# Another assignment of the model dimension to partitions in a gated cross-attention kernel

## The chip, the cores and the metric

The kernel runs on one core of a Trainium2 chip. Its time is what the device takes for one execution, in microseconds (us); lower is better. A core has five engines with their own instruction queues: PE (TensorE, matrix products), DVE (VectorE), ACT (ScalarE), POOL (GpSimd) and SP (SyncE, which here issues nearly all transfers). [...] DMA engines, sixteen to a core, move data between the main memory and SBUF, the on-chip memory of 128 partitions. Matrix products land in PSUM, in banks.

## The reference

For each of 8 batches, x is 1024 rows of D = 1024, the context ("mem") 64 rows of E = 512. All values are float32.

```python
memory_proj = einsum('bme,de->bmd', memory, W_mem)
scores = einsum('bnd,bmd->bnm', hidden_states, memory_proj) / sqrt(D)
attn = softmax(scores, axis=-1)
memory_context = einsum('bnm,bmd->bnd', attn, memory_proj)
gate_input = concatenate([hidden_states, memory_context], axis=-1)
gate = sigmoid(einsum('bnf,df->bnd', gate_input, W_gate) + b_gate)
fused = hidden_states + gate * memory_context
return rmsnorm(fused, norm_w)
```

W_gate has two halves along f: W1, which multiplies x, and W2, which multiplies the memory context. Since the context is attn times memory_proj, the kernel multiplies memory_proj by W2 once per batch ("mg") and then only applies attn. The large product is x times W1.

## The kernel before

**Layout.** A product on PE sums over partitions. So D has to lie over 128 partitions and KD = 8 chunks, in the same way for every operand that is summed over it: x, W1, W2's rows, and memory_proj ("mp"). Before, element d of D lies on partition d // 8 in chunk d % 8. For W1 and W2 that is a plain load, since a partition's 8 rows lie one after another in memory (`rows_by_chunk`, L103). For x it needs a transpose. x is loaded by `load_xq` (L149) in four DMAs, one to each 32 partitions, so that each group of 32 holds one quarter of the columns for all 512 rows of a step. DVE then transposes blocks of 32 x 32 (`transpose_x`, L239, instruction L248), and its input takes every eighth column (`chunks`, L107), so the elements that it reads one after another are 32 bytes apart. `store_mp` (L412, instruction L418) does the same in the other direction for memory_proj, there with the output 32 bytes apart. In the product pm = W_mem times the context (L211 on), W_mem is the stationary operand and its columns are also taken eight apart.

**The start.** SP issues, in this order: the context (memq), W_mem (wm; its first 128 rows go through ACT's queue, L128), W2 in eight loads of 512 KB (L134 to L138), W1 in two of 2 MB (L144), norm_w (nw_sb), and later memory_proj's copies to memory (mpd, L404) and the first block of x (L405). PE transposes the context (L194), multiplies it by W_mem (pm), and then runs seven products for mg (pg, `mg_product`, L434) by one level of a Strassen scheme. DVE runs its own queue strictly in program order ("pin", L89). It holds, one after another: memT copies (L199), differences of W2's blocks (`w2_sum`, L389 and L390), a difference of W1's first half (`outer_sum(5, 7, 1)`, L393) with four smaller ones (L394), the copies of pm from PSUM to mpT (L400, shared with ACT), two steps on mpT (s1 and s2, L459), a difference that needs W1's second half (`outer_sum(7, 3, 7)`, L461), the eight transposes of `store_mp`, and then sums of the pg products, transposes of x's first block and more differences of W1. The sums also free PSUM banks for later products.

**The main part.** There are 16 steps q of 512 rows. Each runs seven outer products (ORDER, L527), each of seven inner products kA to kF (kA has two parts), by two levels of the same scheme. POOL and DVE form the operands and add up the results; DVE also does eight transposes for the next step, the softmax, and the gate. A table of slots (`plan`, L530) sets where each of these stands in the queues. SP loads x and stores the output.

**Helpers.** L92 issues every matmul, L95 every elementwise operation of two tensors, on whichever engine is given, and L98 every DMA of SP. So a profile line with L95 is told apart by its tile names: t_w are W2's differences, t, it and w the operands from W1, l, s and a those from x, mpT memory_proj.

Of the kernel before, what the change touches and what calls it, by code (L numbers as in the profile page):

```python
# [15 lines left out]
P = 128  # L16
# [4 lines left out]
def tile_gated_cross_attention_rmsnorm(  # L21
# [38 lines left out]

    nc = tc.nc
    B, N, D = x.shape
    M, E = mem.shape[1:]
# [3 lines left out]
    BM = B * M  # L70
    KD = D // P
    KE = E // P
    H = 512
    C = 256
    NPAIR = BM // P
# [6 lines left out]
    apool = ctx.enter_context(tc.tile_pool(name="apool", bufs=1))  # L82
# [6 lines left out]
    pin = tc.keep_in_program_order  # L89

    def mm(o, lhsT, rhs, start, stop):
        pin(nc.tensor.matmul(o, lhsT, rhs, start=start, stop=stop, skip_group_check=True))  # L92
# [4 lines left out]
    def load(o, i):  # L97
        pin(nc.sync.dma_start(o, i))  # L98

    def t4k(pool, shape, tag, name):  # L100
        return pool.tile(shape, F32, tag=tag, name=name)

    def rows_by_chunk(w, n):  # L103

        return w.rearrange("(p j) f -> p j f", j=n)

    def chunks(t, n):  # L107

        return t.rearrange("p s e -> p (s e)").rearrange("p (m j) -> p j m", j=n)

    banks = [f"b{i}" for i in range(5)]

    def bank(n, shape, name):
        return ps.tile(shape, F32, tag=banks[n % 5], name=name)
# [10 lines left out]
    memq = [t4k(rot, [P, 2, E], "l2", f"memq{i}") for i in range(2)]  # L125
    wm = t4k(xqpool, [P, KE, D], "xq", "wm")
    wmr = w_mem_t.rearrange("(k p) d -> p k d", p=P)
# [2 lines left out]
        load(memq[g], memr[g])  # L130
    load(wm[:, 1, :], wmr[:, 1, :])
    load(wm[:, 2:, :], wmr[:, 2:, :])
    w2r = rows_by_chunk(w_gate_t[D:, :], KD)
    w2 = []  # L134
    for k in range(KD):
        t = t4k(*((gpool, [P, D], "gate") if k < 7 else (apool, [P, D], "s4")), f"w2_{k}")
        load(t, w2r[:, k, :])
        w2.append(t)  # L138

    w1 = [const.tile([P, 4, D], F32, name=f"w1_{h}") for h in range(2)]
    for h in range(2):
        load(w1[h], rows_by_chunk(w_gate_t[:D, :], KD)[:, 4 * h : 4 * h + 4, :])  # L144
    nw_sb = const.tile([P, D], F32, name="nw_sb")
    load(nw_sb, norm_w.partition_broadcast(P))
    xq = {}

    def load_xq(q):  # L149
# [7 lines left out]
    outer_b = {  # L157
        o: w1[h][:, :, c * H : (c + 1) * H]
        for o, h, c in ((1, 0, 0), (7, 0, 1), (2, 1, 0), (3, 1, 1))
    }  # L160

    t_w2 = [const.tile([P, 4, H], F32, tag=f"t{o}", name=f"t{i}_w2") for i, o in ((1, 6), (2, 4))]
    inner_t = {}

    def w1_place(o):

        if o in (5, 6, 4):
            outer_b[o] = const.tile([P, 4, H], F32, tag=f"t{o}", name=f"t{o}")
        inner_t[o] = const.tile([P, 3, 2, C], F32, tag=f"it{o}", name=f"it{o}")
# [17 lines left out]
    def transpose_mem(g):  # L187

        cols = slice(g * (BM // 2), (g + 1) * (BM // 2))
        for k in range(KE):  # L190
            for r in range(2):
                n = 2 * g + r
                pin(
                    nc.tensor.transpose(  # L194
                        pt[k][:, n * P : (n + 1) * P], memq[g][:, r, k * P : (k + 1) * P], ident
                    )
                )
            o = memT[k // 2][:, k % 2, cols]
            pin((nc.scalar.copy if k % 2 else nc.vector.tensor_copy)(o, pt[k][:, cols]))  # L199

    pt = [bank(4, [P, BM], "pt0")]
    pt += [ps_ctx.tile([P, BM], F32, tag="ctx", name=f"pt{k}") for k in (1, 2)]
    pt += [ps.tile([P, BM], F32, tag="sc", name="pt3")]
    for g in range(2):
        transpose_mem(g)
    pm = [bank(j, [P, BM], f"pm{j}") for j in range(5)]
    pm += [ps_ctx.tile([P, BM], F32, tag="ctx", name=f"pm{j}") for j in (5, 6)]
    pm += [ps.tile([P, BM], F32, tag="sc", name="pm7")]
    for k in range(KE):
        for j in range(KD):  # L210
            mm(  # L211
                pm[j],
                chunks(wm[:, k : k + 1, :], KD)[:, j],
                memT[k // 2][:, k % 2, :],
                k == 0,
                k == KE - 1,
            )
# [16 lines left out]
    A, S, L2, O = {}, {}, {}, {}  # L234
# [4 lines left out]
    def transpose_x(q, t, half):  # L239

        key = q, t // 2, half
        if key not in A:
            A[key] = t4k(
                apool, [P, KH, 2 * P], f"a{t // 2 + 1}{half + 1}", f"a{t // 2 + 1}{half + 1}_{q}"
            )
        r = t % 2
        pin(
            nc.vector.transpose(  # L248
                A[key][:, :, r * P : (r + 1) * P],
                chunks(xq[q][:, 4 * t : 4 * t + 4, :], KD)[:, half * KH : (half + 1) * KH],  # L250
            )
        )

    def outer_s(q, n):
        a11, a12, a21, a22 = (A.get((q, r, h)) for r in range(2) for h in range(2))
        if n == 3:
            S[q, 3] = a21
            tt(nc.vector, a21, a11, a21, ALU.subtract)
            return
        s = S[q, n] = t4k(apool, [P, KH, 2 * P], f"s{n}", f"s{n}_{q}")  # L260
        if n == 1:
# [33 lines left out]
    def scores(q):  # L295
# [3 lines left out]
        for k in range(KD):  # L299
            for r in range(2):  # L300
                mm(
                    pst[r * M : (r + 1) * M, :],
                    mpb[:, k, :],
                    A[q, r, k // KH][:, k % KH, :],
                    k == 0,
# [65 lines left out]
    def add_bias(b):  # L371
# [1 line left out]

    KH = KD // 2
    HM = BM // 2
    b11, b12, b21, b22 = (
        [w2[h * KH + k][:, c * H : (c + 1) * H] for k in range(KH)]
        for h in range(2)  # L380
        for c in range(2)
    )
    t1, t2 = ([t[:, k, :] for k in range(KH)] for t in t_w2)

# [12 lines left out]
    mpT = [[t4k(apool, [P, KH, HM], f"a{r + 1}{h + 1}", f"mpT{r}{h}") for h in range(2)] for r in range(2)]  # L397
# [9 lines left out]
    def mp_step(eng, tag, pool, a, b, op):  # L407
        t = t4k(pool, [P, KH, HM], tag, f"mp_{tag}")
        tt(eng, t, a, b, op)
        return t  # L410

    def store_mp(g):  # L412

        r, n = g // 2, g % 2
        mpq = const.tile([P, 4, Q4], F32, tag=f"it{(4, 6, 2, 3)[g]}", name=f"mpq{g}")
        for h in range(2):
            pin(
                nc.vector.transpose(  # L418
                    chunks(mpq, KD)[:, h * KH : (h + 1) * KH],
                    mpT[r][h][:, :, n * P : (n + 1) * P],  # L420
                )
            )
        for i in range(4):
            load(
                mgd[0, g * P : (g + 1) * P, i * Q4 : (i + 1) * Q4].rearrange(
                    "(s c) e -> c s e", c=32
                ),
                mpq[32 * i : 32 * (i + 1), :, :],
            )
# [4 lines left out]
    def mg_product(n, l, r):  # L434
        nonlocal mg_next
        pgs = []
        for t in range(2):
            tag = mg_banks[mg_next % 8]
            mg_next += 1
            pg = (ps_ctx if tag == "ctx" else ps).tile([P, H], F32, tag=tag, name=f"pg{n}_{t}")  # L440
            for k in range(KH):
# [4 lines left out]
    def mg_tile(pool, tag, name):  # L446
        return t4k(pool, [P, 2, H], tag, name)

# [10 lines left out]
    s1 = mp_step(nc.vector, "s1", apool, m21, m22, ALU.add)  # L459
    s2 = mp_step(nc.vector, "s2", apool, s1, m11, ALU.subtract)  # L460
# [12 lines left out]
    for g in (2, 3, 0, 1):  # L473
        store_mp(g)
# [4 lines left out]
    for t in range(4):  # L479
        transpose_x(0, t, 0)  # L480
# [17 lines left out]
    for t in range(2):  # L498
        transpose_x(0, t, 1)
# [7 lines left out]
    for t in (2, 3):  # L507
        transpose_x(0, t, 1)
# [337 lines left out]
```

## Time and profile before

The time is 980.86 us (three runs, 980.78 to 980.89). The profiled execution spans 979.4 us.

| engine | busy us | share of the span |
|---|---|---|
| PE, matmuls | 964.8 | 99% |
| PE, weight loads | 769.8 | 79% |
| DVE | 820.4 | 84% |
| ACT | 324.9 | 33% |
| POOL | 730.5 | 75% |

| group | count | busy us | mean ns |
|---|---|---|---|
| L248 DVE transposes of x, 128x512 | 128 | 137.9 | 1098 |
| L418 DVE transposes of mp, 128x512 | 8 | 7.7 | 1101 |
| pm weight loads, 128x128 | 64 | 20.0 | 314 |

| transfer | loads | KB each | median us from issue to landing |
|---|---|---|---|
| W2 | 8 | 512 | 11.0 |
| W1 | 2 | 2048 | 15.6 |
| x | 64 | 512 | 9.6 |

The first table is over the whole span. A busy share says how much an engine works and not whether anything waits for it. What sets the end is read from the chain of waits, which follows the last instruction back to what released each step. In the second table, the mean is of the single record; records on one engine overlap a little, so the busy time is less than the count times the mean. In the third, a landing time includes the wait behind earlier transfers.

### The profile page before, as it was taken

The page shows a single profiled execution, that of the slowest core. Times are in us where ns is not written, and L with a number is a line of the kernel's source. Part 1 is how long each engine was busy: PE and PEld are TensorE (multiplying, and loading weights), DVE is VectorE, ACT ScalarE, POOL GpSimd, SP SyncE. Part 2 cuts the span into 40 slices and gives each one's busy share as a digit, 9 for nine tenths or more (in the row PEclk, how much of TensorE's full clock was granted, in tenths as well). Part 3 has the DMA queues.
Part 4 walks back from the last instruction along what each step waited for, and adds up shares of the span by engine and source line. Part 5 has one row for each costly group of instructions (what it writes and reads, how often), then busy time and mean ns, then how long its engine had stood idle before and what let it go on. Part 6 is the DMA issues. An engine that isn't in the chain of part 4 may idle for free.

```text
span 979.4 us, 14277 instructions
## 1 busy us (share of the span) xinstructions
PE 964.8 (99%) x4938; PEld 769.8 (79%) x4938; DVE 820.4 (84%) x1487; ACT 324.9 (33%) x602; POOL 730.5 (75%) x881
## 2 busy tenths in 40 slices
PE   9999999999999999999999999999999999999995
PEld 6546888888887888888887888888887888888873
DVE  3888788979797988979797988979797988979787
ACT  1100234151433334151433334151433334151434
POOL 3366877878787877878787877878787877878772
PEclk9999999999999999999999999999999999999998
DMA  9865264482918374482918374482818364482612
GB/s 372 258 153 145 39 120 107 103 188 62 186 65 165 108 141 106 102 190 65 183 65 164 111 138 105 107 184 66 182 65 168 110 136 104 108 184 68 169 65 86
DMA packets 71255, 128.32 MB, mean 131 GB/s; under 512 B 12432, under 2 KB 49296, under 8 KB 70928
## 3 DMA queue, kind: packets, MB, share of 16 engines
q1 hardware_dynamic: 61760, 93.34, 35.3%
q0 software_dynamic: 9280, 33.56, 18.5%
q8 instruction: 39, 0.64, 0.3%
q10 hardware_dynamic: 144, 0.52, 0.2%
q14 instruction: 32, 0.26, 0.1%
HBM read 87.56 MB, written 39.85 MB: 130 GB/s over the span
## 4 chain that ended last, share of the span: by engine, by line
PE 96%; DVE 2%; DMA 1%; issue 0%; ACT 0%; POOL 0%; DVEq 0%; ACTq 0%
PE kA L92 20%; PE pc L92 12%; PE kE L92 11%; PE kF L92 10%; PE kD L92 10%; PE kC L92 10%; PE kB L92 10%; PE psT L92 6%; PE pg L92 5%; PE pm L92 3%; DVE gate L95 1%; DMA memq<-in_mem 1%; DVE gate L660 0%; PE pa L342 0%; PE sc L316 0%
## 5 line engine op out<-in xcount | busy, mean ns | idle before, releaser
L95 POOL TENSOR_TENSOR gate<-gate,u 128x256 f32<-128x256 f32 x336 | 270.4, 835 | 115.7 <-DVE u L95 110.1
L582 ACT ACTIVATE gate<-gate 128x512 f32<-128x512 f32 x128 | 79.0, 629 | 400.1 <-DVE gate L95 400.1
L95 POOL TENSOR_TENSOR l<-a 128x256 f32<-128x256 f32 x128 | 128.9, 1007 | 60.4 <-DVE a L95 55.8
L248 DVE STREAM_TRANSPOSE a<-xq 128x512 f32<-128x512 f32 x128 | 137.9, 1098 | 4.0 <-DMA xq<-in_x 4.0
L92 PE MATMUL pc<-mg,attnT 64*128 64x256 f32 x512 | 127.4, 389 | 0.0
L611 DVE SCALAR_TENSOR_TENSOR gate<-gate,ss,nw_sb 128x512 f32<-128x512 f32 x120 | 126.0, 1060 | 1.1
L92 PE MATMUL kD<-it,l 128*128 128x256 f32 x448 | 115.0, 379 | 0.0
L92 PE MATMUL kB<-it,l 128*128 128x256 f32 x448 | 115.0, 379 | 0.0
L92 PEld LDWEIGHTS pc<-mg,attnT 64*128 64x128 f32 x512 | 90.6, 186 | 29.7 <-issue 21.2
L92 PE MATMUL kA<-w,a 128*128 128x256 f32 x384 | 98.7, 379 | 0.4 <-ACT u L726 0.4
L92 PEld LDWEIGHTS kD<-it,l 128*128 128x128 f32 x448 | 85.1, 190 | 11.6
L92 PEld LDWEIGHTS kB<-it,l 128*128 128x128 f32 x448 | 85.1, 190 | 11.6
L95 DVE TENSOR_TENSOR gate<-gate,pc 128x512 f32<-128x512 f32 x128 | 87.0, 680 | 5.8 <-ACT gate L582 5.8
L95 POOL TENSOR_TENSOR l<-s 128x256 f32<-128x256 f32 x96 | 75.7, 789 | 10.8 <-PE kF L92 10.7
L92 PEld LDWEIGHTS kA<-w,a 128*128 128x128 f32 x384 | 71.6, 190 | 10.2 <-ACT u L726 0.8
L726 ACT COPY u<-kA 128x256 f32<-128x256 f32 x112 | 40.5, 362 | 102.1 <-PE kA L92 99.9
L92 PE MATMUL kE<-it,a 128*128 128x256 f32 x256 | 69.0, 392 | 0.0
L95 DVE TENSOR_TENSOR u<-u,kB 128x256 f32<-128x256 f32 x112 | 45.5, 406 | 28.1 <-PE kB L92 24.9
L92 PE MATMUL kA<-t,s 128*128 128x256 f32 x256 | 67.4, 386 | 0.0
L92 PE MATMUL kC<-w,l 128*128 128x256 f32 x256 | 65.7, 379 | 0.0
L92 PE MATMUL kF<-w,l 128*128 128x256 f32 x256 | 65.7, 379 | 0.0
L596 ACT ACTIVATE junk<-gate 128x1024 f32<-128x1024 f32 x60 | 63.5, 1059 | 2.1 <-DMA gate<-in_x 1.2
(123 smaller groups left out, 1996.6 us busy)
## 6 DMA issues: line engine op xcount, KB each, us to landing
xq<-in_x SPq DMA_DIRECT2D x64, 512.0 KB, 9.6
gate<-in_x POOLq DMA_DIRECT2D x60, 512.0 KB, 7.8
out<-gate SPq DMA_DIRECT2D x60, 512.0 KB, 2.6
w<-in_w_gate_t SPq DMA_DIRECT2D x8, 512.0 KB, 11.0
w<-in_w_gate_t SPq DMA_DIRECT2D x2, 2048.0 KB, 15.6
mg<-mgd SPq DMA_DIRECT2D x16, 256.0 KB, 4.0
mpd<-mpT SPq DMA_DIRECT2D x4, 512.0 KB, 3.8
mgd<-mpq SPq DMA_DIRECT2D x16, 128.0 KB, 2.6
```

The costliest lines, as they stand in the source:

```text
L92: pin(nc.tensor.matmul(o, lhsT, rhs, start=start, stop=stop, skip_group_check=True))
L95: pin(eng.tensor_tensor(o, a, b, op))
L248: nc.vector.transpose(A[key][:, :, r * P : (r + 1) * P], chunks(xq[q][:, 4 * t : 4 * t + 4, :], KD)[:, half * KH : (half + 1) * KH],)
L582: pin(nc.scalar.activation(g, g, AF.Sigmoid))
L596: nc.scalar.activation(junk, O[q, t], AF.Square, accum_out=ss[:, t % 2 : t % 2 + 1])
L611: nc.vector.scalar_tensor_tensor(g[:, cols], g[:, cols], rstd[:, t % 2 : t % 2 + 1], nw_sb[:, cols], ALU.mult, ALU.mult,)
L726: pin(nc.scalar.copy(p1, kb["A"]))
```

## The change

The change assigns D differently: element d, written as d = 256 i + 32 j + r with i below 4, j below 8 and r below 32, now lies on partition 32 i + r in chunk j. Groups of 32 columns that lie together in memory stay together. A transposed block of x then reads 32 neighbouring elements and writes 32 neighbouring elements, in place of elements 32 bytes apart. The purpose is a cheaper DVE transpose of x and of memory_proj.

All operands have to follow. A load of a chunk of W2 or W1 now takes 4 blocks of 32 rows, 256 rows apart, to all 128 partitions, in one DMA with two row strides; for W1 there are eight of them in place of two. W_mem's columns are put in that order by four DVE copies (`order_wm`), the first ahead of the context's transposes, the others behind them, and pm reads the copies.

```diff
-    def rows_by_chunk(w, n):
-        return w.rearrange("(p j) f -> p j f", j=n)
-    def chunks(t, n):
-        return t.rearrange("p s e -> p (s e)").rearrange("p (m j) -> p j m", j=n)
+    def rows_by_chunk(w):
+        return w.rearrange("(i j r) f -> i r j f", i=4, r=32)
+    def blocks(t, half):
+        return t.rearrange("p s (j r) -> p s j r", r=32)[:, :, half * KH : (half + 1) * KH, :]
+    def tokens(t):
+        return t.rearrange("p j (s c) -> p s j c", c=32)
...
-        load(t, w2r[:, k, :])
+        load(t, w2r[:, :, k, :])
...
-    for h in range(2):
-        load(w1[h], rows_by_chunk(w_gate_t[:D, :], KD)[:, 4 * h : 4 * h + 4, :])
+    w1r = rows_by_chunk(w_gate_t[:D, :])
+    for k in range(KD):
+        load(w1[k // KH][:, k % KH, :], w1r[:, :, k, :])
...
+    def order_wm(k):
+        t = t4k(apool, [P, KD, P], ("a11", "a12", "s1", "s2")[k], f"wmp{k}")
+        pin(
+            nc.vector.tensor_copy(
+                t.rearrange("p j (i r) -> p j i r", r=32),
+                wm[:, k, :].rearrange("p (i j r) -> p j i r", i=4, r=32),
+            )
+        )
+        wmp.append(t)
+
+    order_wm(0)
     for g in range(2):
         transpose_mem(g)
+    for k in range(1, KE):
+        order_wm(k)
...
-                chunks(wm[:, k : k + 1, :], KD)[:, j],
+                wmp[k][:, j, :],
...
             nc.vector.transpose(
-                A[key][:, :, r * P : (r + 1) * P],
-                chunks(xq[q][:, 4 * t : 4 * t + 4, :], KD)[:, half * KH : (half + 1) * KH],
+                tokens(A[key][:, :, r * P : (r + 1) * P]),
+                blocks(xq[q][:, 4 * t : 4 * t + 4, :], half),
             )
...
                 nc.vector.transpose(
-                    chunks(mpq, KD)[:, h * KH : (h + 1) * KH],
-                    mpT[r][h][:, :, n * P : (n + 1) * P],
+                    blocks(mpq, h),
+                    tokens(mpT[r][h][:, :, n * P : (n + 1) * P]),
                 )
```

More of the change, by code (lines that the diff above doesn't have):

```diff
@@ L72, in tile_gated_cross_attention_rmsnorm @@
     KE = E // P
+    KH = KD // 2
     H = 512
@@ L132, in tile_gated_cross_attention_rmsnorm @@
     load(wm[:, 2:, :], wmr[:, 2:, :])
-    w2r = rows_by_chunk(w_gate_t[D:, :], KD)
+    w2r = rows_by_chunk(w_gate_t[D:, :])
     w2 = []
@@ L203, in tile_gated_cross_attention_rmsnorm @@
     pt += [ps.tile([P, BM], F32, tag="sc", name="pt3")]
+    wmp = []
+    def order_wm(k):
[8 more added lines that the diff above has]
+    order_wm(0)
     for g in range(2):
         transpose_mem(g)
+    for k in range(1, KE):
+        order_wm(k)
     pm = [bank(j, [P, BM], f"pm{j}") for j in range(5)]
@@ L372, in add_bias @@
         pin(nc.gpsimd.dma_start(mgs[b][M:P, :], b_gate.partition_broadcast(M), accum_op=ALU.add))
-    KH = KD // 2
     HM = BM // 2
```

## The prediction, made before the changed kernel was run

> **What bounds the kernel now.** I read the chain of waits first, then who TensorE (PE) waits for, then the start in order of time, because that is where the loads of the weights stand.
>
> ```profile
> PE 96%; DVE 2%; DMA 1%; issue 0%; ACT 0%; POOL 0%; DVEq 0%; ACTq 0%
> ```
> ```profile
> PE kA L92 <- ACT u L726: 1.6, 3, 1.1
> PE pz L92 <- DVE zeros L118: 1.2, 1, 1.2
> PE pt L194 <- DMA memq<-in_mem: 0.8, 1, 0.8
> PE pt L194 <- DVE memT L199: 0.3, 1, 0.3
> ```
>
> The chain is PE from the first microseconds to the tail, and all PE waits (us in total, times, longest) sum to 3.9 us. So busy time taken from the vector engine (DVE) is worth almost nothing; only something that stops PE moves the end. In the first 84 us PE lives on what DVE prepares, and DVE on DMA:
>
> ```profile
> 12.57 0.69 DVE L95 TENSOR_TENSOR t_w<-w 128x512 f32<-128x512 f32 x1 [3.69 <-DMA w<-in_w_gate_t]
> ...
> 20.32 3.17 DVE L95 TENSOR_TENSOR t_w<-w,t_w 128x512 f32<-128x512 f32 x2 [0.19 <-DMA w<-in_w_gate_t]
> 26.42 2.29 DVE L95 TENSOR_TENSOR t<-w 128x2048 f32<-128x2048 f32 x1 [2.92 <-DMA w<-in_w_gate_t]
> ...
> 31.16 0.75 DVE L400 COPY mpT<-pm 128x256 f32<-128x256 f32 x2
> ...
> 39.67 2.29 DVE L95 TENSOR_TENSOR w<-w,w 128x2048 f32<-128x2048 f32 x1
> ```
> ```profile
> 54.91 4.09 DVE L248 STREAM_TRANSPOSE a<-xq 128x512 f32<-128x512 f32 x4 [4.02 <-DMA xq<-in_x]
> ```
> ```profile
> 36.36 33.90 PE pg L92 x79
> ```
> ```profile
> GB/s 0 194 299 397 426 404 421 407 412 415 404 415 407 500 360 513 360 492 382 440 333 57 41 310 10 274 340 316 195 238 188 186 218 189 189 214 378 333 240 292
> ```
>
> Columns: start, length, instruction, idle time before it and its releaser. DVE consumes each block of W2 as it lands (12.57 to 20.32), then W1's first half (26.42), and only then copies PE's pm results into mpT (31.16), which PE needs for its next products, pg, at 36.36. The last line is bandwidth in steps of 1.5 us: the weights run at 400 to 440 GB/s until about 31 us. The front is fed by DMA with 4 to 10 us to spare, no more.
>
> [...] Before, both sides of the W loads begin with 128[...] (DMA share 1.03 from 12 to 20 us). No DMA of this trace begins with a dimension below 16[...].
> [...] L248 reads with a step of 32 bytes and its 128x512 transposes take 1098 ns, against 692 ns for a 128x512 add.
> [...] the first ten matmul passes of 256 columns take 4.25 us, 0.43 each, where four of kA's later take 0.86, 0.22 each.
>
> **The change, part by part.**
> 1. W2 and W1 loads. The source becomes (4 blocks, 32 rows, 1024), the target 128 partitions. [...] Sixteen loads of 524,288 bytes take this form (W1's two of 2 MB become eight). Price at 16 engines: the starts 12.57 to 20.32 span six loads, 1.29 us each, 406 GB/s or 25.4 per engine. At 4 engines: 4 x 1.29 = 5.17 us each. Load n lands at 11.28 + 5.17n: W2's last (n=8) at 52.6, W1's first half (n=12) at 73.3 instead of 26.42, the second half (n=16) at 94.0. Bounds: [...] 10% below the trace's rate would be 5.7 us.
> 2. First path, to PE's products. DVE is in order: outer_sum(5,7,1) of L393 waits for W1's first half, and the mpT copies of L400 are queued behind it. From its start to them it took 31.16 - 26.42 = 4.74 us: 78.0. First copy 0.4: PE resumes at 78.5, having stood since pm ended at 36.4; it loses 42.1. The seven products ran from 36.36 to kA at 84.43, 48.1 us, so kA at 126.6; [...]: **128.3**.
> 3. Second path. outer_sum(7,3,7) of L461 (39.67 before) waits for W1's second half at 94.0. Behind the weights in the same four engines' queues come nw_sb, the mpd stores and x's first block: per engine 32, 131 and 131 KB, at 25.4 GB/s 1.3 + 5.2 + 5.2 us, so x lands at 105.7; with the median 10.0 us that such a load took from issue to landing, about 110. I take 108. From the first transposes of x (54.91) to the sums that free the PSUM banks of kA (four of the six adds that begin at 75.58, 0.6 each, so 78.1) DVE worked 23.2 us without a gap; six transposes in it save up to 0.41 each, leaving 20.8: **128.8**, with ends 126.5 and 133. The last two products ask for nothing late: their PSUM banks are free at about 94.0 + 2.3 + 7.7 + 1.3 = 105 (after the sum, eight transposes, two adds) and 108 + 4.1 + 1.2 = 113, and PE reaches them at 114 and 121.
> 4. Transposes (128 of x, 8 of mp). Both sides now have 32 neighbours in a row. Bounds: 1098 ns (no gain) and the add's 692; I take 692, 56 us of DVE. On the path none of it counts but the 2.4 above: PE's matmuls hide the rest.
> 5. order_wm, four copies of 128x1024. [...] the trace has 1225 ns for a 128x1024 add. I take the latter[...]. The first waits for wm's first rows (issue 0.74, landing 4.6 later): 5.3 to 6.6, before DVE's first memT copy at 6.68. The other three have finished by about 14, before PE asks for the second block at 15.5. Behind them stand the W2 differences, which wait longer now. Cost zero.
> 6. pm's weight loads shrink (313 ns towards 190). pm's matmuls step at 433 ns, so they are hidden.
>
> Sum: kA starts at 128.8 instead of 84.43, +44.4; the steady part has 0.5 us of PE waits between 70 and 960 us, so nothing comes back. 980.86 + 44.4 = 1025.3, I say **1025**.
>
> **Rivals.**
> A, the loads keep all engines (the source's two dimensions treated as 128 rows): landings as before, the rest hidden, 980.9 to within 0.5. For it: every load in the trace runs on all engines, and 128 targets could be dealt out. [...] 8%.
> B, as A, and the shorter transposes also end PE's waits: at most 1.6 + 0.8 + 0.3 = 2.7 us, **978.2**. Against: of these only kA's can depend on DVE's load. 5%.
> C, four engines[...]: **1017**. [...] 20%.
> D, four engines at 5.7 us each, or x later: halves at 79.7 and 102.5, x at 116.5, kA at about 138: **1034**. [...] 17%.
> My forecast: 50%.
>
> **How the numbers follow.** Four engines have 87%, all of them slower. The range 1013 to 1039 holds C and D with 4 to 5 us of room and leaves out A, B and the outermost of C and D, together some 18%. Slower 0.87, same 0.08 (A), faster 0.05 (B).
>
> **What would show it.** Right: W loads with landings some 5 us apart, bandwidth near 102 GB/s from 12 to 90 us, DVE waiting for W at L95 and PE idle about 42 us before pg, x landing after 100, transposes near 0.7 us, a main part of the old length (84.4 to 979.4). Wrong: W landings still 1.3 us apart, which is A or B. Were the landings slow and PE yet started before 70, step 2's queue would be misread; were kA later than 133, step 3's.

## The result and the profile after

The changed kernel takes 1034.45 us (median of five, 1032.43 to 1036.78) against 980.87 in the same runs: ratio 1.0545, interval 1.0528 to 1.0562. Some executions are in a slower state of the core, and ratios are of the others alone, which matters only for e4 below, where two of four executions are left out.

The shares of the chain that ended last, by engine (SPq is SP's queue, at work on issuing transfers), and then PE's waits (us in total, times, longest):

```profile
PE 85%; SPq 5%; DVE 4%; DMA 4%; issue 1%; ACT 0%; POOL 0%; DVEq 0%; ACTq 0%
```
```profile
PE pg L92 <- ACT mpT L420: 41.8, 1, 41.8
PE pg L92 <- DVE w L95: 5.0, 2, 4.7
PE kB L92 <- DVE gate L95: 2.3, 1, 2.3
PE kA L92 <- ACT u L746: 1.6, 3, 1.1
PE pz L92 <- DVE zeros L122: 1.2, 1, 1.2
```

Three waits are new: 41.8, 5.0 and 2.3 us, all in the first 155 us. DVE's queue in order of time shows what stands behind the first two:

```profile
16.83 0.69 DVE L95 TENSOR_TENSOR t_w<-w 128x512 f32<-128x512 f32 x1 [4.76 <-DMA w<-in_w_gate_t]
21.85 0.69 DVE L95 TENSOR_TENSOR t_w<-w 128x512 f32<-128x512 f32 x1 [4.33 <-DMA w<-in_w_gate_t]
...
52.04 0.69 DVE L95 TENSOR_TENSOR t_w<-w,t_w 128x512 f32<-128x512 f32 x1 [4.33 <-DMA w<-in_w_gate_t]
71.95 2.29 DVE L95 TENSOR_TENSOR t<-w 128x2048 f32<-128x2048 f32 x1 [19.21 <-DMA w<-in_w_gate_t]
...
76.69 2.74 DVE L420 COPY mpT<-pm 128x256 f32<-128x256 f32 x8
...
93.41 2.29 DVE L95 TENSOR_TENSOR w<-w,w 128x2048 f32<-128x2048 f32 x1 [10.13 <-DMA w<-in_w_gate_t]
...
110.50 2.49 DVE L269 STREAM_TRANSPOSE a<-xq 128x512 f32<-128x512 f32 x4 [8.86 <-DMA xq<-in_x]
...
118.06 5.69 DVE L95 TENSOR_TENSOR w<-w,t_w 128x512 f32<-128x512 f32 x4
```

W2's eight blocks land 5.03 us apart, (52.04 - 16.83) / 7, in place of 1.29. W1's halves land at 71.95 and 93.41, x's first block at 110.5. How many DMA engines worked is read from the bandwidth by stretch: the last two numbers are the mean busy share of the 16 engines and GB/s.

```profile
15.00:50.00 35.00, 20.73 (x49) 8.90 (x47) 4.85 (x7) 0.00 (x0) 5.34 (x3) 0.87 0.26 104
```

A share of 0.26 is 4.2 engines of 16, and 104 GB/s is 26 for each of four. The mean alone could also be sixteen engines that are busy a quarter of the time. The start and length of each packet in the trace settle it: four packets were at work at once for 90% of this stretch and five for the rest, never fewer than four; in the kernel before, from 12 to 20 us, sixteen or more. PE's products around the waits, and then kA's first ones in the kernel before:

```profile
77.57 9.09 PE L92 MATMUL pg<-w,mpT 128*128 128x512 f32 x16 [41.84 <-ACT mpT L420]
...
118.79 4.64 PE L92 MATMUL pg<-w,mpT 128*128 128x512 f32 x6 [4.67 <-DVE w L95]
123.80 4.56 PE L92 MATMUL pg<-w,mpT 128*128 128x512 f32 x10 [0.37 <-DVE w L95]
...
135.07 1.03 PE L92 MATMUL kA<-w,a 128*128 128x256 f32 x4
```
```profile
84.27 1.03 PE L92 MATMUL kA<-w,a 128*128 128x256 f32 x4
```

kA begins at 135.07 and not at 84.27, 50.8 us later. The spans differ by 1032.7 - 979.4 = 53.3; 2.35 of what is left is the single kB wait. What the change was for did come. The group of x's transposes before and after:

```profile
L248 DVE STREAM_TRANSPOSE a<-xq 128x512 f32<-128x512 f32 x128 | 137.9, 1098 | 4.0 <-DMA xq<-in_x 4.0
```
```profile
L269 DVE STREAM_TRANSPOSE a<-xq 128x512 f32<-128x512 f32 x128 | 86.0, 692 | 8.9 <-DMA xq<-in_x 8.9
```

A transpose takes 692 ns and not 1098, and DVE saves 137.9 - 86.0 = 52 us on x. Its whole busy time fell by less, from 820.4 to 780.8: the copies of W_mem came in (2.7 us), and some adds took longer (the sixteen `s<-a,a` 27.1 us in place of 21.3).

### The profile page after: what moved, and what is told of

The parts are those of the page before. It is cut to its first block, busy times and chain, and to the rows that moved or that the text cites. A ratio compares the mean times of both kernels' runs of the same rounds, so it can differ in the third digit from the quotient of the medians.

```text
span 1032.7 us, 14290 instructions
## 1 busy us (share of the span) xinstructions
PE 969.8 (94%) x4938; PEld 763.1 (74%) x4938; DVE 780.8 (76%) x1491; ACT 324.6 (31%) x602; POOL 732.4 (71%) x881
## 4 chain that ended last, share of the span: by engine, by line
PE 85%; SPq 5%; DVE 4%; DMA 4%; issue 1%; ACT 0%; POOL 0%; DVEq 0%; ACTq 0%
PE kA L92 18%; PE pc L92 11%; PE kE L92 10%; PE kF L92 9%; PE kD L92 9%; PE kB L92 9%; PE kC L92 9%; PE psT L92 6%; SPq L98 5%; DMA w<-in_w_gate_t 2%; PE pg L92 2%; DVE gate L95 1%; DMA xq<-in_x 1%; DVE w L95 1%; DVE t L95 0%
## 5 line engine op out<-in xcount | busy, mean ns | idle before, releaser
L95 POOL TENSOR_TENSOR l<-a 128x256 f32<-128x256 f32 x128 | 124.7, 974 | 65.9 <-DVE a L95 57.2
L92 PE MATMUL pc<-mg,attnT 64*128 64x256 f32 x512 | 127.4, 389 | 0.0
L269 DVE STREAM_TRANSPOSE a<-xq 128x512 f32<-128x512 f32 x128 | 86.0, 692 | 8.9 <-DMA xq<-in_x 8.9
L92 PE MATMUL pg<-w,mpT 128*128 128x512 f32 x48 | 25.3, 683 | 46.9 <-ACT mpT L420 41.8
```

Of the source, the lines that this page charges most:

```text
L95: pin(eng.tensor_tensor(o, a, b, op))
L269: nc.vector.transpose(tokens(A[key][:, :, r * P : (r + 1) * P]), blocks(xq[q][:, 4 * t : 4 * t + 4, :], half),)
```

## The experiments

The theory: the loads in four blocks use 4 of 16 DMA engines, and this late landing, carried to PE by DVE's ordered queue and by x's landing, is the whole loss. The rivals: two row strides are slow as such, 4 KB pieces are, or the new order of x and of W_mem costs something.

**e2: the loads alone, in the kernel before.**

```diff
-        return w.rearrange("(p j) f -> p j f", j=n)
+        return w.rearrange("(i j r) f -> i r j f", i=4, r=32)
...
-        load(t, w2r[:, k, :])
+        load(t, w2r[:, :, k, :])
...
-    for h in range(2):
-        load(w1[h], rows_by_chunk(w_gate_t[:D, :], KD)[:, 4 * h : 4 * h + 4, :])
+    w1r = rows_by_chunk(w_gate_t[:D, :], KD)
+    for k in range(KD):
+        load(w1[k // 4][:, k % 4, :], w1r[:, :, k, :])
```

> The kernel before with one part of the change alone: W2 and W1 loaded by DMAs of 4 blocks of 32 rows (so the weights' rows come in another order than x's and the output isn't the reference's). Theory: landings 5 us apart, 1033 to 1039, a little above the changed kernel since the first transposes of x after its late landing take 1.02 us each in a row and not 0.62. Rival (the loss needs the new layout of x or the copies of W_mem): 980 to 983.

1035.97 us, ratio 1.0561 (1.0546 to 1.0577). Landings are again 5.03 us apart, and PE's waits are the same two, with the third absent:

```profile
PE pg L92 <- ACT mpT L401: 42.0, 1, 42.0
PE pg L92 <- DVE w L95: 7.4, 1, 7.4
```

The loads alone make the loss. The new transposes and the copies of W_mem are not needed for it. The second wait is even longer, 7.4 against 5.0, with the first four transposes of x in it, which take 1098 ns each on average in e2 and not 692.

**e3: two strides, with the 32 outermost.** As e2, with one letter order changed:

```diff
-        return w.rearrange("(i j r) f -> i r j f", i=4, r=32)
+        return w.rearrange("(i j r) f -> r i j f", i=4, r=32)
```

> As e2, still two row strides to all 128 partitions and the same 4 KB rows in 16 DMAs, but the dimension of 32 rows is outermost and the 4 blocks are inner (other order of rows, output not the reference's). Theory (only the size of the outermost dimension matters, 32 gives 16 engines): landings 1.3 us apart, 980 to 983. Rival (two strides as such are slow, or rows spread over memory are): landings 5 us apart, 1033 to 1039. Rival (W1 in 4 KB pieces costs by itself): 983 to 988.

981.46 us, ratio 1.0005 (0.9997 to 1.0014). The stretch from 12 to 20 us:

```profile
12.00:20.00 8.00, 8.00 (x20) 5.80 (x20) 4.55 (x7) 0.00 (x0) 2.54 (x2) 1.00 1.03 411
```

All engines, 411 GB/s, and W2's blocks 1.29 us apart again. Neither the two strides, nor the 4 KB pieces, nor sixteen loads in place of ten cost anything that the time shows; which dimension stands outermost decides in these runs.

**e4 and e10: eight outermost.** As e2 with i=8 and r=16; in e10 `"(j r i) f -> i r j f"`, so that the eight groups begin one row apart and not 128.

> As e2 (the kernel before with only the loads of W2 and W1 changed, rows in another order than x's, output not the reference's), but in 8 blocks of 16 rows instead of 4 of 32. Theory (the outermost size is the number of engines, 8): landings 2.5 us apart, W1's first half at 42, PE back at 47.5, kA at 96 to 99, time 991 to 997. Rival (a load of more than one row stride is slow whatever the size of its outermost dimension): as e2, 1034 to 1038. Rival (there is a fixed cost for each piece and not a rate for each engine): 981 to 985.

> As e4, 8 outermost and 16 inner, but the 8 groups begin one row (4 KB) apart in memory and step 8 rows, in place of 128 rows (512 KB) apart and one row steps (rows in another order, output not the reference's). The targets on chip are those of e4. e4's landings were 4.2 us apart, not 2.5: about 16 GB/s for each of 8 engines. If the distance of the sources made that: 2.5 us apart and 991 to 997. If the targets did[...]: about 4 us apart, 1000 to 1022, with a wide spread again.

```profile
15.00:50.00 35.00, 20.93 (x49) 14.78 (x48) 5.54 (x8) 0.00 (x0) 7.09 (x4) 0.87 0.52 125
```
```profile
15.00:50.00 35.00, 20.99 (x49) 14.84 (x48) 5.54 (x8) 0.00 (x0) 7.09 (x4) 0.87 0.51 126
```

The first line is e4's, the second e10's. A share of 0.52 is eight engines, as e4's theory had it, and eight packets were at work at once for some 80% of both stretches, more for the rest. But they moved 125 GB/s, 15.6 each where four engines moved 26 each: landings 4.2 us apart and not 2.5. The median times are 1013.48 and 1017.35 us and the ratios 1.0251 (1.0206 to 1.0297) and 1.0344 (1.0306 to 1.0382). Single executions range from 1001.6 to 1021.8 and from 1009.0 to 1021.3, and both profiles are of the slowest one. So 15.6 is a figure of these two executions. e4's fastest lost 20.8 us to the kernel before where the profiled one lost 41, so its loads probably came sooner, which no trace here shows. My number for e4 was a miss all the same, since no execution came within 991 to 997. The count of engines was right, a fixed rate for each was wrong.

e10 rules out the distance between the sources as the cause. That the targets are the cause was not shown by any run. The cause stays open.

**e1: a load to each 32 partitions.** The changed kernel with

```diff
-        load(t, w2r[:, :, k, :])
+        for i in range(4):
+            load(t[32 * i : 32 * (i + 1), :], w2r[i][:, k, :])
```

and W1 likewise, in eight loads.

> The changed kernel, with W2 and W1 loaded by one DMA to each 32 partitions, whose source begins with 32 rows: 32 DMAs of 128 KB and 8 of 512 KB; all else as in the changed kernel. Theory (the four-block form of the loads confines each to 4 of 16 engines, and that is the whole loss): W2 lands at the old pace of about 1.3 us a chunk, W1's first half by 29, kA begins at 84 to 86, time 979.5 to 982.5. Rival (the order of W_mem's columns, the new transposes or another phase of DVE and POOL cost something too): above 985 with the weights landing early. Rival (many DMAs bind SP's issue): W1's first half after 32 and a time of 983 to 990.

992.28 us, ratio 1.0113 (1.0097 to 1.0130): most of the loss is gone, not all. The stretch from 20 to 30 us, and PE's first wait:

```profile
20.00:30.00 10.00, 10.00 (x25) 4.40 (x24) 2.84 (x5) 0.00 (x0) 5.36 (x4) 1.00 1.05 232
```
```profile
PE pg L92 <- ACT mpT L422: 9.1, 1, 9.1
```

All engines are busy and move 232 GB/s, where loads to 128 partitions moved 411. W1's first half lands at 39.6 and PE stands 9.1 us. None of my three cases said this: I had thought of SP's issue and not of a lower rate with all engines at work. The size of a load isn't the cause: e1's loads of W1 have 512 KB each, as W2's had in the kernel before at 410 GB/s, and moved 216 GB/s from 36 to 45 us. Each of e1's loads has 32 target partitions, but its source rows changed too, and no run changed the target alone, so that the 32 partitions are the cause was not shown.

**e6: the two halves of the partitions on two queues.** As e1, with the loads of partitions 64 to 127 issued by ACT.

> As e1 (a load to each 32 partitions), with the loads of the lower 64 partitions on SP's queue and those of the upper 64 on ACT's, behind ACT's first copies, so that the engines have work for two groups of partitions at once. Theory (e1's 230 GB/s is the limit of 32 partitions as a target, since all engines were busy at half their rate, and not SP's issue or the size of a load): weights at 380 GB/s or more, W1's first half by 31, kA at 84 to 87, time 979.5 to 983. Rival (loads of 128 KB are slow by themselves): still near 230 GB/s and 990 to 994.

991.97 us, ratio 1.0113 (1.0098 to 1.0128), so e1's time; the theory lost. The time is that of the rival, but its reason isn't shown, since e1's loads of 512 KB were as slow as those of 128 KB. The 128 KB loads of W2 (10 to 20 us) and then the 512 KB loads of W1 (36 to 45 us):

```profile
10.00:20.00 10.00, 10.00 (x25) 4.45 (x24) 3.15 (x5) 0.00 (x0) 0.00 (x0) 1.00 1.06 237
...
36.00:45.00 9.00, 0.71 (x1) 0.50 (x2) 6.29 (x10) 1.13 (x4) 0.00 (x0) 0.67 1.03 300
```

W2 gained nothing (237 GB/s; e1: 240 in the same stretch), W1 some (300; e1: 216). Why only W1 gained was not shown.

**e5: x's first block on ACT's queue.** The changed kernel, with `load_xq(0)` issued by ACT behind the context's copies.

> The changed kernel, with the first block of x issued from ACT's queue early in the front, behind no weights; the weights stay in the four-block form. Theory (after W1's second half, kA waits for x's late landing, then DVE's queue up to the difference that overwrites a block of W2): x lands before 40, the product that waited 4.7 us waits at most 1.5, kA begins at 127.5 to 130 instead of 135, time 1026 to 1030. Rival (x's landing is beside the path and W1's second half alone sets it): kA at 134 to 136, time 1032 to 1036.

1039.11 us, ratio 1.0593 (1.0577 to 1.0608), slower where I expected 1026 to 1030. Nor did x land before 40 us: ACT issued its four loads only between 12.2 and 67.8 us. The wait in question did vanish, though:

```profile
PE pg L92 <- ACT mpT L421: 55.7, 1, 55.7
PE kA L92 <- ACT u L746: 1.6, 3, 1.1
PE pz L92 <- DVE zeros L122: 1.2, 1, 1.2
```

PE runs from 91.8 to kA at 142.08 without a stop. But with x's 2 MB issued among the weights some W landings came 6 to 8 us apart and not 5.03, and W1's first half landed at 86.18, 14.2 later. A load of x taken out of SP's queue delayed the weights all the same.

**e8: the transposes of x behind the difference of b21.** The changed kernel with

```diff
-    for t in range(4):
-        transpose_x(0, t, 0)
-    for part in range(2):
-        inner_s(0, 1, part)
...
     w2_sum(nc.vector, b21, b21, t2)
+    for t in range(4):
+        transpose_x(0, t, 0)
+    for part in range(2):
+        inner_s(0, 1, part)
```

> The changed kernel, with the first four transposes of x and the operands made of them put behind the difference that overwrites a block of W2 (b21), in DVE's and POOL's queues. Theory (after W1's second half the end is set by a chain that the prediction missed: x lands late, the transposes wait for it, the difference of b21 is queued behind them, and the sixth product reads b21): the 5 us of PE waits before that product vanish, kA at 127.5 to 130 instead of 135, time 1026 to 1030. Rival (x's late landing holds kA by another way, through its own operands): kA stays at 133 to 136, time 1031 to 1036.

1025.56 us, ratio 1.0455 (1.0440 to 1.0471). PE's only long wait is the first one, and kA begins at 127.35:

```profile
PE pg L92 <- ACT mpT L420: 42.0, 1, 42.0
PE kA L92 <- ACT u L746: 1.6, 3, 1.1
```
```profile
127.35 1.03 PE L92 MATMUL kA<-w,a 128*128 128x256 f32 x4
```

The waits before the sixth product are gone. So the second chain is shown: x's landing held DVE, behind DVE's transposes stood the difference of b21, and the sixth product reads b21.

**e9: e6 with two groups of DVE's work moved back.** `outer_sum(5, 7, 1)` and `inner_sums(nc.vector, 1)` go behind the mpT copies and the steps s1 and s2; the transposes move as in e8.

> e6 (a load to each 32 partitions on two queues) with two groups of DVE's work moved back: the difference that waits for W1's first half and its four smaller ones go behind the mpT copies and the two steps on mpT, and the first four transposes of x go behind the difference of b21, as in e8. Theory (what is left of the loss in e1 and e6 is only that the mpT copies, and so PE, stand behind a difference of W1 in DVE's queue): PE passes from pm to pg without a wait, kA at 84 to 86, time 979.5 to 982.5. Rival (W1's late landing at 230 to 300 GB/s still holds PE later on, through x or the second half): 984 to 990.

981.34 us, ratio 1.0005 (0.9996 to 1.0013). PE's waits are those of the kernel before (to within 0.1 us), and kA begins at 84.16:

```profile
PE kA L92 <- ACT u L754: 1.6, 3, 1.1
PE pz L92 <- DVE zeros L122: 1.2, 1, 1.2
PE pt L201 <- DMA memq<-in_mem: 0.9, 1, 0.9
PE pt L201 <- DVE memT L206: 0.3, 1, 0.3
```

```profile
PE 964.5 (98%) x4938; PEld 761.8 (78%) x4938; DVE 775.3 (79%) x1491; ACT 324.6 (33%) x602; POOL 732.1 (75%) x881
```

This is the new layout with W2 and W1 loaded in other pieces and two groups of DVE's work moved, and so without the loss in the front: DVE works 775.3 us in place of 820.4, and the time is that of the kernel before within its interval. The cheaper transposes are worth nothing here, since in the kernel before PE didn't wait for them. No version beat the kernel before.

## Why the prediction was right, and where not

The direction, the mechanism and the range held: 1034.45 in 1013 to 1039, 9 us above the 1025 forecast. The range was set by other rates of the loads and a later x (C and D); that it also held the chain that step 3 missed was partly luck. kA later than 133 was the prediction's own sign of a misread step 3, and kA began at 135.07. By its steps:

1. **Loads.** Four engines, which no trace of the kernel before showed, were measured (share 0.26, four packets at once, and e3 as the counter-test). 5.17 us a load predicted, 5.03 measured; halves of W1 at 73.3 and 94.0 predicted, 71.95 and 93.41 measured. Rivals A and B fall with this, and so do the other rates of C (faster engines, which no run showed) and D (5.7 us a load). The time is D's 1034, but it came about by step 3 and not by D's slower engines.
2. **First path.** DVE's queue held the mpT copies as described; PE back at 78.5 predicted, 77.57 measured. e9 confirms the queue as the cause, at its own landings: with the difference behind the copies PE does not wait, where in e6 it waited 8.3 us. The 1.7 us between 126.6 and 128.3 were an estimate of mine for a slower restart. The first product after the idle time took 9.1 us against 7.0 usual, so 2.1; the granted clock was 0.50 from 77.5 to 81 us and 1.00 from 83 on.
3. **Second path, the step that failed.** x landed at 110.5, not 108, and "The last two products ask for nothing late" was false. I had looked for the PSUM banks of these products and not for their operands: the sixth reads b21, which DVE overwrites by a difference that stands behind the waiting transposes. 110.5 to 123.75 is that queue (2.49 + 1.25 + 2.85 + 1.27 + 5.69, less small overlaps). It cost the 5.0 us of waits and, after PE had stood again, some 2 us at a slower pace (9.2 us for the sixth product and not 7.0, at a mean granted clock of 0.91 from 110 to 130 us); 128.8 became 135.07. Of these 6.3 us x's own lateness is a part: 110.5 + 20.8 = 131.3 by the prediction's path. e8 takes this away and lands at 127.4 and 1025.56.
4. **Transposes.** 692 ns, as taken. With x late they shorten the second path, as said (a wait of 5.0 us and not e2's 7.4); with quick loads they are of no worth (e9). They saved 54.7 us of the 56 forecast, 2.8 of it on memory_proj, though DVE's busy time fell by only 39.6.
5. **order_wm.** 692 ns each (median, 128x1024), and not the 1225 I took: as long as an add of half as many elements (692 for 128x512). Hidden, as said.
6. **pm's weight loads.** 190 ns, hidden, as said.

"The steady part has 0.5 us of PE waits, so nothing comes back" left out that something could be added. In the profiled execution one kB waits 2.35 us for DVE, which had been held in an add that usually takes 0.69:

```profile
149.98 3.85 DVE L95 TENSOR_TENSOR it<-w,it 128x512 f32<-128x512 f32 x1
```

POOL ran adds from 148.9 on almost without a gap, until 154.4. What made the add longer was not shown. The kB groups of e5, e8 and e9 have no such wait.

Together: 44.4 was forecast for the start of kA, 50.8 measured (6.3 from step 3 and the rest from small terms), and 2.35 for kB.

## What to carry to other kernels

Look at the outermost dimension of every load before changing a layout: here a view that splits 128 rows into 4 blocks of 32 left twelve of sixteen engines without work, although the bytes, the pieces and the number of loads stayed the same (share 0.26 in e2 against 1.03 in e3). Cheaper work on an engine that nobody waits for bought nothing (45 us of DVE in e9), while a later landing in the front goes through every ordered queue behind it; so before calling a wait hidden, list for each held instruction all that is queued behind it, operands as well as buffers. And where a transfer must be late, first move the work that needs it behind the work that does not: e8 and e9 got back 9 and 11 us by order alone.

## What the runs showed of the hardware that I had not expected

- The engines of a DMA did not have one rate in these runs. Four engines over 128 target partitions moved 26 GB/s each, eight 15.6 (in the slowest executions of e4 and e10), sixteen 25.7 (e3), and sixteen with loads to 32 partitions 14.5 (e1). The packets show the same: one of 4 KB took 159 ns with four engines, 164 in e3, 294 in e4, 278 in e10 and 294 in e1 (medians of the stretches shown above). Why eight are slower stays open.
- SP's issue slowed with the landings: in the changed kernel its sixteen weight loads took from 2.8 to 73.6 us to issue, 4.8 us each (median), where the ten before took from 2.8 to 14.2. x stands in the same queue behind norm_w and the stores of memory_proj, which need the late mpT copies, and was issued only from 91.2 on.
- The first block of x, four loads in 1 KB pieces, has 2 MB, by my estimate 131 KB for each of sixteen engines, as much as a weight load of 512 KB is for each of four. It cost the weights 14.2 us (e5), where such a weight load takes 5.03.
